# The fold's x2 rows loaded one slot of work, or one block of columns, sooner into the same two buffers

## The chip, the cores and the metric

One core of a Trainium2 chip. The metric is device time in microseconds (us) of one execution. Several runs of one kernel are told by their median and their lowest and highest.

## The reference

2,048 tokens (2 x 1,024) of width 1,024 go through two feed-forward layers, each followed by an addition of its input and a layer norm. All numbers are float32.

```python
s = silu(x @ w_gate.T)                     # 2752 columns
s[the 1376 smallest |s| of each row] = 0
x = layernorm(x + (s * (x @ w_up.T)) @ w_down.T)

def lin(x, wq, A, B):                      # wq has a quarter of the columns of w
    return x @ tile(wq, (1, 4)).T + 0.5 * (x @ A.T @ B.T)
h = silu(lin(x, w1q, a1, b1)) * lin(x, w3q, a3, b3)      # rank 2
x = layernorm(x + lin(h, w2q, a2, b2))
```

Since the second layer's weight is one block repeated four times, `x @ w.T` needs only the sum of the four quarters of `x`. That sum is the fold: four pieces of 256 columns of a row are added to one.

## The kernel before, in words

The tokens are 16 tiles of 128 rows, in four groups of four (GT). Every float32 operand is split into a high part (a cast to the matmul type) and a low part (the rest), and each product is made of three matmuls. The stages are:

- **gate_up**, to 932 us: gate and up projections of all groups, with the results stored in DRAM scratch (s_d, m_d), while topk finds the mask bytes (k_d).
- **down** (line 612), group by group: six blocks of inner columns (DB: 512, 512, 512, 384, 384, 448) times four tiles. For each block and tile, down_load (702) loads a piece m of m_d and a piece u of k_d; down_mask (725) casts u to ub on ScalarE (728) and multiplies m by it on GpSimd (729); down_prep (735) transposes m on TensorE (749), copies the high part mh on ScalarE (753) and subtracts the low part ml on VectorE (754); down_mm (778) runs the matmuls (769) and adds the result to the accumulator on VectorE (772). down_w (675) brings the block's weights: either the split pair wh, wl from scratch (688), or raw rows wr (607) that are cast on ScalarE (175) and subtracted on GpSimd (176). After the last block the accumulator is normalised and stored to x_d (793).
- Beside the **last group of down**, whose matmuls end at 1462 us, run two generators, each one step per tile of work. ffn_consts makes `br` in eight pieces of 344 columns: six tiny loads into `braw` (816) after a memset (812), a cast (175), a subtraction (176) and two small DMAs from ScalarE's queue (819). f1_first (655) does two things for t = 0 to 3: it loads the rows of tile t + 8 into an `x2a` buffer (660) for four dot products on VectorE (663), and then calls f1_tile(t) and f1_tile2(t).
- **f1_tile** (921) is the fold. It takes an x2a buffer, loads tile t's rows from x_d into it on SyncE's queue (926), adds the four quarters in three GpSimd instructions (933 to 935) into `fold`, and fills `tl` (939 to 946). **f1_tile2** (949) transposes fold and tl on TensorE (955, 957), copies to fh on ScalarE (960) and makes fl on VectorE (961). There are two x2a buffers, shared by lines 660 and 926, and one fold buffer, which line 663 also uses for its throw-away output.
- **ffn** (860), per group: eight blocks of 344 columns (NB); in blocks 0, 2, 4, 6 the folds of the next group's four tiles are made. f1_mm (964) makes the gate and up products (987 to 990), f2_prep and f2_mm the way back, layer norm and output.

The order in which an engine or a queue runs its instructions isn't that of the source. A planner that estimates durations orders them when the program is built, within the data dependences and a few orders that the source asks for: `load_behind` keeps a load behind the last load of m (714) that was issued, `behind` keeps work behind the last casts. Each engine and queue then runs its list strictly in order, and an instruction that waits holds up those behind it. Each load or store is given one of eight completion counters in turn (SyncE's and ScalarE's alike), and waits until the earlier transfer with that counter has landed; so eight are in flight at most, and a big one holds up the eighth after it.

Of the kernel before, what the change touches and what calls it, by code (L numbers as in the profile page):

```python
# [7 lines left out]
F = mybir.dt.float32  # L8
# [10 lines left out]
P = 128  # L19
H = 1024  # L20
# [5 lines left out]
NB = NI // BW  # L26
# [6 lines left out]
GT = 4  # L33
# [19 lines left out]
class Ring:  # L53
    def __init__(self, n, slots, dt):
        self.n, self.slots, self.dt = n, slots, dt
# [10 lines left out]
class Kern:  # L66
    def __init__(self, tc, A, O):
        self.tc, self.nc, self.A, self.O = tc, tc.nc, A, O
        self.nt = A["xt"].shape[0]
        self.x_seen = False  # L70
        self.lasta = self.lastv = self.lastd = None
        self.pend = self.lastp = None
        self.cache, self.wd_d, self.wd_g, self.wst = {}, {}, {}, []

    def run(self):
# [536 lines left out]
    def down(self, g, f1=None, early=0):  # L612
        n, ea = 0, []
        for ib in range(len(DB)):
            if f1 is not None:
                if ib == f1:
                    self.fg = self.f1_first()
            ws = []
            for t in range(g * GT, (g + 1) * GT):
                st = {"e": n} if n < early else {}  # L620
                load = lambda: self.down_load(st, ib, t, n)
                prep = lambda st=st, ib=ib: self.down_prep(st, ib)
                mm = lambda st=st, ib=ib, t=t, ws=ws: self.down_mm(st, ib, t, ws)
                if n < early:
                    load()
                    ea.append((self.pend, prep))
                    self.q2.append(mm)
                    if n == early - 1:
                        for j in range(2):
                            yield  # L630
                            with self.behind():
                                for e in ea:
                                    e[j]()
                        self.pend = None
                        yield
                else:
                    self.masks()
                    self.item(lambda: (load(), self.down_w(g, ib, ws)), prep, mm, 2, 3)
                n += 1
                if g == 0 and n == 12:  # L640
                    self.tkg = self.topk(self.nt // GT - 1, 2)
                if (n > 11 or g) and self.tkg and next(self.tkg, 1):
                    self.tkg, self.dg = None, self.dots_down()
                if f1 is not None and n > 4:
                    next(self.fcg, None)
                    if ib >= f1:
                        next(self.fg, None)
                for _ in range(2 if n % 2 else 1):
                    next(self.dg, None)
        if f1 is not None:  # L650
            list(self.fg)
            self.masks()
        yield

    def f1_first(self):
        for t in range(GT):
            f, x2 = self.f1_room()
            jk, o = f.bitcast(U8), t + 2 * GT
            with self.load_behind():
                self.nc.sync.dma_start(x2, self.x_d[o])  # L660
            for i in range(4):
                with self.behind():
                    self.nc.vector.scalar_tensor_tensor(
                        jk, x2, 0.5, self.abc[:, i, :], ALU.mult, ALU.mult, accum_out=self.dall[:, o, i : i + 1]
                    )
                if i < 3:
                    yield
            self.f1_tile(t, f)
            yield
            self.f1_tile2(t)  # L670
# [189 lines left out]
    def ffn(self, g):  # L860
        tiles = [t for t in range(g * GT, (g + 1) * GT) if t < self.nt]
        for b in range(NB):
            ws = []
            if tiles[-1] + 1 < self.nt:
                if b % 2 == 0:
                    if b:
                        self.f1_tile2(tiles[-1] + b // 2)
                    self.f1_tile(tiles[-1] + 1 + b // 2)
            for t in tiles:
                self.item(  # L870
                    lambda: self.f1_prep(b, ws),
                    lambda: None,
                    lambda st=self.fst[t], b=b, ws=ws: self.f1_mm(st, b, ws),
                    2, 2,
                )
        if tiles[-1] + 1 < self.nt:
            self.f1_tile2(tiles[-1] + GT)
        ws = []
        for t in tiles:
            self.item(  # L880
                lambda: self.f2_w(ws),
                lambda t=t: self.f2_prep(self.fst[t], t),
                lambda st=self.fst[t], t=t, ws=ws: self.f2_mm(st, t, ws),
                2, 1,
            )
# [20 lines left out]
    def f1_prep(self, b, ws):  # L906
        nc, fp = self.nc, self.fp
        bs = slice(b * BW, (b + 1) * BW)
        if not ws:
# [8 lines left out]
                nc.sync.dma_start(ab[:, r, :], self.A["a2"][r : r + 1, bs].partition_broadcast(P))  # L918
            ws.append(ab)

    def f1_tile(self, t, f=None):
        nc, fp, sm = self.nc, self.fp, self.sm
        V, G = nc.vector, nc.gpsimd
        st = self.fst[t] = {}
        x2 = fp.tile([P, H], F, tag="x2a", bufs=2, name="x2a")
        nc.sync.dma_start(x2, self.x_d[t])
        d = self.dall[:, t]
        f = f or fp.tile([P, 2 * P], F, tag="fold", bufs=1, name="fold")
        for i in range(4 if t >= 3 * GT else 0):
            pr = self.fp2.tile([P, H], F, tag="pr", bufs=2, name="pr")  # L930
            V.tensor_tensor(pr, x2, self.abc[:, i, :], ALU.mult)
            nc.scalar.activation(pr, pr, AF.Copy, scale=0.5, accum_out=d[:, i : i + 1])
        G.tensor_tensor(f, x2[:, 0:256], x2[:, 256:512], ALU.add)
        G.tensor_tensor(f, f, x2[:, 512:768], ALU.add)
        G.tensor_tensor(f, f, x2[:, 768:1024], ALU.add)
        dr = sm.tile([P, 4], R, tag="dr", name="dr")
        V.tensor_copy(dr, d)
        tl = fp.tile([P, P + 6], F, tag="tl", bufs=1, name="tl")
        G.memset(tl, 0.0)
        d2 = d.rearrange("p (w r) -> p w r", w=2)  # L940
        dr2 = dr.bitcast(F).rearrange("p (w r) -> p w r", w=2)
        for w in range(2):
            q = 38 * w
            V.tensor_copy(tl[:, q : q + 2], dr2[:, w])
            V.tensor_copy(tl[:, q + 2 : q + 4], dr2[:, w])
            V.tensor_tensor(tl[:, q + 4 : q + 6], d2[:, w], dr2[:, w], ALU.subtract)
        st["f"] = f, tl
# [150 lines left out]
```

## Time and profile before

| | us |
|---|---|
| runs, median (lowest to highest) | 1917.42 (1915.79 to 1919.49) |
| profiled execution, its own time | 1919.06 |
| its span, first to last instruction | 1917.3 |
| TensorE matmul busy | 1882.4 (98%) |
| VectorE, ScalarE, GpSimd busy | 1226.0, 910.2, 991.2 |
| mean granted TensorE clock | 0.994 |
| DMA moved | 485.51 MB, mean 253 GB/s |

How to read it: the first 20 us of a span of 1917.3 us and any other 20 us look alike at 98%, so the place of the missing 2% is read from tables over stretches and from the list of waits. A row of that list names the waiting engine, its operation and line, what it waited for, and then the total in us, how many times, and the longest one. In a timeline a row has its start, its duration, the engine, the line, the operation, the tiles, and in brackets the idle time before it with what ended it. SPq and ACTq are the issue of a DMA by SyncE's and ScalarE's sequencers: their time is the issue (with the gaps between merged ones), not the transfer.

### The profile page before, as it was taken

How to read it: one execution, taken by the hardware profiler on the slowest of the kernel's cores; microseconds unless marked ns; L12 is line 12 of the kernel's file. 1: busy time of each engine (PE TensorE's matmuls, PEld its weight loads, DVE VectorE, ACT ScalarE, POOL GpSimd, SP SyncE). 2: the span in 40 equal slices, each digit the busy share in tenths (PEclk: the TensorE clock that was granted, in tenths of full speed). 3: DMA queues.
4: the chain of work that ended last, by engine and by line, in shares of the span. 5: the costliest groups of instructions: out<-in, count | busy, mean ns of one | idle time of the engine just before them, and what ended most of it. 6: DMA issues, size and time to landing. Idle time of an engine off the chain costs nothing. (4 is left out here: it accounts for less than half of the span.)

```text
span 1917.3 us, 29389 instructions
## 1 busy us (share of the span) xinstructions
PE 1882.4 (98%) x10825; PEld 1752.9 (91%) x10825; DVE 1226.0 (64%) x1831; ACT 910.2 (47%) x1454; POOL 991.2 (52%) x612
## 2 busy tenths in 40 slices
PE   9999999999999999999999999999999999999998
PEld 9999999999999999999888888888777979898896
DVE  4623546667368574591249998687567857779565
ACT  4333468424783258622256633323333746567362
POOL 5665664345445344355566564543665836436062
PEclk9999999999999999999999999999999999999999
DMA  7677687676977868677687867977777878485651
GB/s 269 235 251 258 241 312 269 215 265 250 337 240 224 315 237 307 232 236 260 236 317 246 288 216 258 341 232 271 254 240 256 275 288 322 148 319 179 228 198 66
DMA packets 165341, 485.51 MB, mean 253 GB/s; under 512 B 24676, under 2 KB 45284, under 8 KB 165192
## 3 DMA queue, kind: packets, MB, share of 16 engines
q1 hardware_dynamic: 164984, 483.29, 72.4%
q8 instruction: 85, 1.39, 0.3%
q14 instruction: 64, 0.52, 0.1%
q10 hardware_dynamic: 208, 0.31, 0.0%
HBM read 367.15 MB, written 116.33 MB: 252 GB/s over the span
## 5 line engine op out<-in xcount | busy, mean ns | idle before, releaser
L176 POOL TENSOR_TENSOR wl<-wr,wh 128x1376 fp32r<-128x1376 f32 (+2 forms) x193 | 582.3, 3025 | 471.4 <-ACT wh L175 422.8
L355 PE MATMUL mm<-wh,xh 128*128 128x344 f32 x1928 | 611.0, 322 | 3.3 <-DMA wh<-tw3T1h 3.3
L355 PE MATMUL mm<-wh,xl 128*128 128x344 f32 x1928 | 610.4, 320 | 0.0
L175 ACT CAST wh<-wr 128x1376 fp32r<-128x1376 f32 (+2 forms) x198 | 238.3, 1210 | 350.9 <-PE mm L355 167.0
L355 PEld LDWEIGHTS mm<-wh,xh 128*128 128x128 f32 x1928 | 365.1, 189 | 3.6 <-issue 3.6
L355 PEld LDWEIGHTS mm<-wh,xl 128*128 128x128 f32 x1928 | 364.9, 189 | 0.0
L355 PE MATMUL mm<-wl,xh 128*128 128x344 f32 x1928 | 342.6, 320 | 0.0
L355 PEld LDWEIGHTS mm<-wl,xh 128*128 128x128 f32 x1928 | 310.8, 188 | 0.0
L769 PE MATMUL mm<-wh,mh 128*128 128x512 f32 x680 | 218.1, 401 | 0.5 <-ACT mh L753 0.5
L769 PE MATMUL mm<-wl,mh 128*128 128x512 f32 x680 | 214.6, 395 | 0.6 <-POOL wl L176 0.5
L769 PE MATMUL mm<-wh,ml 128*128 128x512 f32 x648 | 203.7, 394 | 0.8 <-DVE ml L754 0.8
L462 ACT ACTIVATE jk<-a,cur 128x2752 int8<-128x2752 f32 x66 | 170.8, 2588 | 29.0 <-DVE cur L492 19.8
L1000 POOL TENSOR_TENSOR hf<-hf,gt 128x344 f32<-128x344 f32 x96 | 142.2, 1491 | 75.3 <-DVE gt L994 68.4
L729 POOL TENSOR_TENSOR m<-m,ub 128x512 f32<-128x512 f32 (+2 forms) x93 | 112.0, 1205 | 115.7 <-ACT ub L728 63.7
L987 PE MATMUL mm<-wh,fh 128*128 128x344 f32 x512 | 166.5, 326 | 5.0 <-DVE gt L994 4.8
L989 PE MATMUL mm<-wh,fl 128*128 128x344 f32 x512 | 164.3, 321 | 0.0
L988 PE MATMUL mm<-wl,fh 128*128 128x344 f32 x512 | 164.3, 321 | 0.0
L769 PEld LDWEIGHTS mm<-wl,mh 128*128 128x128 f32 x680 | 127.0, 188 | 29.1 <-POOL wl L176 1.2
L772 DVE TENSOR_TENSOR acc<-acc,mm 128x1024 f32<-128x1024 f32 x96 | 116.5, 1213 | 54.4 <-PE mm L769 36.2
L769 PEld LDWEIGHTS mm<-wh,ml 128*128 128x128 f32 x648 | 121.1, 188 | 27.5 <-DVE ml L754 1.0
L769 PEld LDWEIGHTS mm<-wh,mh 128*128 128x128 f32 x680 | 123.5, 188 | 24.6 <-ACT mh L753 1.2
L998 ACT ACTIVATE pa<-pa 128x344 f32<-128x344 f32 x256 | 123.0, 483 | 36.4 <-DVE pa L996 31.7
(191 smaller groups left out, 2734.6 us busy)
## 6 DMA issues: line engine op xcount, KB each, us to landing
wr<-wu SPq DMA_DIRECT2D x64, 688.0 KB
wr<-wg SPq DMA_DIRECT2D x52, 688.0 KB
wr<-wd SPq DMA_DIRECT2D x54, 512.0 KB
s_d<-cc SPq DMA_DIRECT2D x64, 344.0 KB
m_d<-mt SPq DMA_DIRECT2D x64, 344.0 KB
a<-s_d SPq DMA_DIRECT2D x64, 344.0 KB
wl<-wc_w SPq DMA_DIRECT2D x48, 344.0 KB
wh<-wc_w SPq DMA_DIRECT2D x48, 344.0 KB
```

Source lines behind the costliest of these rows:

```text
L175: self.lasta = self.nc.scalar.copy(hi, raw)
L176: (eng or self.nc.gpsimd).tensor_tensor(lo, raw, hi.bitcast(F), ALU.subtract)
L355: self.nc.tensor.matmul(o, l, r, start=start and n < m and n % (2 * KH) == 0, stop=stop and n >= m and (n - m) % KH == KH - 1)
L462: nc.scalar.activation(jk.bitcast(I8), av[j], AF.Sign, bias=t, scale=-1.0, accum_out=s)
L729: nc.gpsimd.tensor_tensor(m[:, :w], m[:, :w], ub[:, :w], ALU.mult)
L769: nc.tensor.matmul(ps[:, h], a, b[:, h * 512 : (h + 1) * 512], start=i == 0, stop=i == len(ops) - 1)
L772: nc.vector.tensor_tensor(out, out, ps.rearrange("p a b -> p (a b)"), ALU.add)
L987: nc.tensor.matmul(o, fh[:, c, :], wh[:, c, :], start=c == 0, stop=False)
L988: nc.tensor.matmul(o, fh[:, c, :], wl[:, c, :], start=False, stop=False)
L989: nc.tensor.matmul(o, fl[:, c, :], wh[:, c, :], start=False, stop=False)
L998: nc.scalar.activation(pa[:, r], pa[:, r], AF.Copy, scale=0.5, accum_out=part[:, r, b : b + 1])
L1000: G.tensor_tensor(hf[:, hs], hf[:, hs], gt, ALU.add)
```

## The change

The allocation of x2a and its load leave f1_tile and become a function of their own, f1_x, which keeps the buffer in a dictionary until f1_tile takes it. The calls:

- in f1_first, f1_x(t) comes right after the load of tile t + 8, three steps ahead of f1_tile(t);
- at the end of the last down, f1_x(4);
- in ffn, f1_x for the next tile in the odd block ahead of its fold, and in block 7 for the first tile of the group after.

The load in f1_x stands in load_behind. There are still two buffers, taken in the same order, and the same 16 loads.

```diff
@@ down
         if f1 is not None:
             list(self.fg)
             self.masks()
+            self.f1_x(GT)
         yield
@@ f1_first
             with self.load_behind():
                 self.nc.sync.dma_start(x2, self.x_d[o])
+            self.f1_x(t)
             for i in range(4):
@@ ffn
                     if b:
                         self.f1_tile2(tiles[-1] + b // 2)
                     self.f1_tile(tiles[-1] + 1 + b // 2)
+                elif b < NB - 1:
+                    self.f1_x(tiles[-1] + 1 + (b + 1) // 2)
+                else:
+                    self.f1_x(tiles[-1] + GT + 1)
@@
+    def f1_x(self, t):
+        if t < self.nt:
+            self.xn[t] = self.fp.tile([P, H], F, tag="x2a", bufs=2, name="x2a")
+            with self.load_behind():
+                self.nc.sync.dma_start(self.xn[t], self.x_d[t])
+
     def f1_tile(self, t, f=None):
...
-        x2 = fp.tile([P, H], F, tag="x2a", bufs=2, name="x2a")
-        nc.sync.dma_start(x2, self.x_d[t])
+        x2 = self.xn.pop(t)
```

More of the change, by code (lines that the diff above doesn't have):

```diff
@@ L72, in __init__ @@
         self.pend = self.lastp = None
+        self.xn = {}
         self.cache, self.wd_d, self.wd_g, self.wst = {}, {}, {}, []
```

## The prediction

> **What bounds the kernel now.** The page first: it says that TensorE is the bound nearly everywhere, at full clock.
>
> ```profile
> PE 1882.4 (98%) x10825; PEld 1752.9 (91%) x10825; DVE 1226.0 (64%) x1831; ACT 910.2 (47%) x1454; POOL 991.2 (52%) x612
> PEclk9999999999999999999999999999999999999999
> ```
>
> So a change to loads can only be worth what TensorE idles near them. The table over stretches of 20 us (span; TensorE, weight loads, VectorE, ScalarE, GpSimd busy; granted clock; DMA share; GB/s) shows where that is: in the last down, where the folds of tiles 0 to 7 are made.
>
> ```profile
> 1340.00:1360.00 20.00, 20.00 (x96) 16.34 (x95) 7.96 (x9) 5.89 (x9) 11.04 (x7) 1.00 0.78 283
> 1360.00:1380.00 20.00, 16.83 (x79) 13.26 (x78) 9.26 (x14) 6.48 (x11) 12.12 (x12) 1.00 0.68 241
> 1400.00:1420.00 20.00, 18.99 (x87) 15.09 (x86) 14.75 (x22) 5.08 (x11) 11.88 (x12) 1.00 0.68 219
> 1420.00:1440.00 20.00, 18.75 (x89) 15.18 (x89) 13.63 (x24) 6.61 (x11) 12.52 (x16) 1.00 0.83 302
> 1440.00:1460.00 20.00, 17.77 (x83) 13.72 (x83) 14.13 (x36) 5.68 (x8) 12.87 (x15) 1.00 0.76 258
> 1460.00:1480.00 20.00, 17.55 (x88) 15.90 (x88) 16.05 (x51) 7.91 (x17) 11.03 (x16) 0.83 0.69 233
> ```
>
> From 1360 to 1480, TensorE lacks 10.6 us of 120 (3.17, 0.51, 1.01, 1.25, 2.23 and 2.45 by stretch; the second is not shown). The last row adds a clock of 0.83: 0.17 x 20 = 3.4 us lost besides. Next, TensorE's rows that waited, from its timeline:
>
> ```profile
> 1407.68 0.55 PE L749 MATMUL tp<-ident,m 128*128 128x128 f32 x3 [0.37 <-DVE ml L754]
> 1413.03 0.52 PE L749 MATMUL tp<-ident,m 128*128 128x128 f32 x3 [0.65 <-DVE ml L754]
> 1424.47 0.44 PE L955 MATMUL tp<-ident,fold 128*128 128x128 f32 x2 [1.25 <-POOL fold L935]
> 1451.35 0.55 PE L749 MATMUL tp<-ident,m 128*128 128x128 f32 x3 [1.16 <-DVE fl L961]
> 1472.92 0.69 PE L955 MATMUL tp<-ident,fold 128*128 128x128 f32 x2 [1.87 <-POOL fold L935]
> ```
>
> No row waits for x2a itself. The waits for fold are waits for GpSimd. What holds GpSimd is seen in SyncE's list of waits from 1376 to 1426 and in the timelines of SyncE and ScalarE:
>
> ```profile
> SPq L816 <- DMA wh<-wd2048h: 4.1, 1, 4.1
> SPq L926 <- DMA br<-braw: 2.8, 1, 2.8
> SPq L688 <- DMA x2a<-x_d: 1.5, 1, 1.5
> ```
> ```profile
> 1393.50 0.38 SPq L715 DMA_DIRECT2D u<-k_d  x1
> ...
> 1397.70 0.32 SPq L926 DMA_DIRECT2D x2a<-x_d  x1
> ...
> 1401.89 0.35 SPq L688 DMA_DIRECT2D wh<-wd1920h  x1
> ...
> 1411.37 0.35 SPq L714 DMA_DIRECT2D m<-m_d  x1
> ```
> ```profile
> 1411.82 0.48 ACT L753 CAST mh<-tp 128x384 fp32r<-128x384 f32 x1 [7.53 <-DMA wl<-wd2048l]
> ```
>
> Read them as one chain. The load of tile 2 (1397.70) waited 2.8 us for a counter. The weights wd1920 waited for that load to land (1.5 us, to 1401.89). Their four transfers landed by 1411.13 (landing records of the trace). The last tiny braw load waited 4.1 us for one of them. ScalarE's br DMA waited for another, with mh behind it, 7.53 us late. VectorE's ml follows, and TensorE stops at 1413.03. The m load at 1411.37 is late too, so its mask, the next ones and the fold behind them on GpSimd are late, and TensorE stops at 1424.47.
>
> **The change, part by part.** I number the masks of the two 384-wide blocks 1 to 8.
>
> *ffn and the end of down.* Nothing is added or removed: 16 loads of 512 KB, 0.32 us of issue each. In the orders of the two programs, SyncE's queue is the same from the w3 rows of ffn's block 0 on. The planner had already put the 12 loads of tiles 4 to 15 as early as a buffer is free. So they don't move: 0, with nothing that must hide it.
>
> *Tile 0.* Same place (1342.83): 0.
>
> *Tile 1.* Its load goes from 1382.32 to some 1376.3, ahead of two m/u pairs; its buffer is free, since fold 0 ended at 1372.9. The fold doesn't gain: it began at 1394.00, and the load had landed at 1386.45. The pairs behind get a counter later, up to 1.3 us each (u of mask 4 waits for wd1664h, landed 1382.26, instead of issuing at 1381.01). Their masks ran at 1384.58 and 1386.57, and TensorE took them at 1391.92 and 1398.24, so over 5 us of other matmuls hide it: 0. Without that cover it would cost the 1.3 us.
>
> *Tile 2, the edit that counts.* Its load now stands right behind the load of tile 10, ahead of an m and of six braw loads. Two u rows and another m that stood ahead of it (1393.50 to 1394.82) go behind the weights and twelve braw loads. The load waits for fold 1's last add, which ended at 1396.36; at 1397.70 it had waited for more than that. And by its new place the counter that wd1920 waits for is a tiny braw load's. From 1396.4: x2a and m 0.8, six braw loads 2.1 (1398.27 to 1400.33), so wd1920 issues at about 1399.3 instead of 1401.89. If fold 1 is earlier, as its masks' loads are, up to 1.5 us better still. At 1.3 us a transfer (four landed at 1.3 us steps, 1361.48 to 1365.55), with 2.9 us to the first, the weights have landed by some 1406.2 instead of 1411.13.
>
> Queued behind them is now u of mask 7: issue 1406.3, landed 2.0 us later (as the u of 1411.82 did, at 1413.83). ScalarE's list has its cast (0.51) ahead of mh of mask 5 (0.48), and then comes ml (0.56): 1409.9. TensorE needs that at 1412.4. So the waits of 0.65 and, less surely, 0.37 go. The second stands behind VectorE rows that ran 3.43 us (L663 at 1399.14, median 1.22) beside GpSimd's subtraction, so I bound it by 0 and 0.37.
>
> The fold of tile 2: GpSimd's row 933 came at 1417.76, behind a mask at 1416.76 and a braw subtraction at 1412.98 that waited for ScalarE. These move up by about 3 us. VectorE's last dot product (1415.54 to 1416.79) still bounds it. From there the three adds and what lies between took 6.65 us, 1.15 of it a wait for the next u: end 1422.3 to 1423.4 instead of 1424.41. TensorE asked at 1423.22, less what was gained before. So 0.5 to 1.25 of that wait goes. Sum for tile 2: 1.2 to 2.3 us; I take 2.2, because the trace has the whole chain moving by more than each wait is long.
>
> *Tile 3.* Its load in fact moves a place later, behind a row of w3. It landed at 1434.12, the fold began at 1442.65: 0, with 8 us of cover.
>
> *Behind it, 1448 to 1453.* TensorE waited 0.25, 1.16 and 0.77 for ScalarE and VectorE, which were at the splits of the w3 and w1 rows (ScalarE idle 7.97 us for these, until 1446.53). If those rows come as much earlier as TensorE does, the waits stay: 0. If the loads gain more, all 2.18 go. If they gain less, it may cost as much as TensorE gained, 2.2. The loads stand behind the same backlog, which begins 2 to 3 us earlier, so I take the middle of the first two: 1.1.
>
> *At 1470 to 1473* the wait stays. One fold buffer makes tile 6's transposes, three adds (2.3 us) and tile 7's transposes a row of steps, and tile 7's load was issued at 1460.23. [...] The trace differs: with gaps of 0.39 and 1.87 the clock fell to 0.83 of 20 us, while 1.69 and 1.48 between 1360 and 1380 left it at 1.00. [...]
>
> **Sum.** 2.2 + 1.1 = 3.3 us. The profiled execution took 1919.06 us, its span 1917.3 with 1.8 around it: it would take 1915.8. It stands 1.6 us above the median of the runs. From the median, 1917.42 - 3.3 = 1914.1.
>
> **The rivals.**
>
> *The u row comes too late (slower).* The saving hangs on wd1920 moving up. If it stays at 1401.89, because the fold, the braw memsets on GpSimd or a counter hold SyncE's queue as long as before, the weights land at 1411.13, u of mask 7 at 1413.2, and then 0.51, 0.48 and 0.56 give ml at 1414.8. ScalarE's cast of u has blocked mh behind it. TensorE waits from 1412.8 (the planner put two more matmuls ahead): 2.0 instead of 0.65, so 1.3 more. A stall of 2 us may also halve the clock as at 1472, another 3.4: 1917.42 + 4.7 = 1922.1, or 1918.7 without. It decides when that u lands after about 1411.3. For it: ScalarE's queue is strict, and u gives up a lead of 12 us. Against it: the waits of 2.8 and 1.5 us that vanish.
>
> [...]
>
> *The change does nothing (same).* The gain is given back in ffn's first group, where the DMA queues are near full and TensorE already waits 2.83 us at 1546.57 for ScalarE: 1917.4, give or take 1.5. Against it: that wait stands in a chain of ScalarE, VectorE and GpSimd work that moves along with TensorE.
>
> **How the numbers follow.** About 0.2% (3.8 us) is what a measurement of this kernel can tell from no change; faster ends at 1913.6, slower begins at 1921.3. Main case 0.40, own range 1912.3 to 1915.8: 0.17 faster, 0.23 same. Late u row 0.27: 0.21 slower, 0.06 same. Clock case 0.15, all faster. Nothing 0.18, all same. Together 0.32, 0.47 and 0.21. The range reaches from 1910.3, about the middle of the clock case, to 1922.2, the far price of the late u row.
>
> **What would show it.** Right: wd1920 issued by 1399.5 or so, no wait of line 688 for x2a, the 7.53 of line 753 and TensorE's 0.65 and 1.25 gone, and the ffn stretches as before, only earlier. Wrong: line 728 of ScalarE waiting for u near 1411 with mh behind it, a longer wait of line 749, or a granted clock below 1.00 between 1400 and 1440. The clock row of 1460 to 1480 tells the third case. I would be most wrong if the planner's new order makes another engine's list wait where I followed only SyncE's.

## The result, and the profile after

| | before | changed |
|---|---|---|
| median (lowest to highest), 22 runs each, taken together | 1916.69 (1911.59 to 1919.99) | 1919.65 (1912.12 to 1927.18) |
| ratio, 95% interval | | 1.0019 [1.0010, 1.0028] |
| profiled execution, its own time (span) | 1919.06 (1917.3) | 1920.05 (1918.2) |

The change makes the kernel 0.19% slower. The forecast was 3.3 us less; it became about 3 us more. The page shows almost nothing: TensorE's busy time is the same, and the clock row has an 8 in one slice (1439 to 1487 us).

```profile
PE 1882.7 (98%) x10825; PEld 1753.0 (91%) x10825; DVE 1229.8 (64%) x1831; ACT 910.7 (47%) x1454; POOL 988.2 (52%) x612
PEclk9999999999999999999999999999998999999999
```

The table over stretches says where. These are the rows that were shown of before:

```profile
1360.00:1380.00 20.00, 17.00 (x81) 13.23 (x80) 9.76 (x17) 7.06 (x12) 13.55 (x13) 1.00 0.72 250
1400.00:1420.00 20.00, 20.00 (x93) 16.30 (x93) 14.17 (x23) 5.67 (x12) 11.60 (x14) 1.00 0.84 270
1420.00:1440.00 20.00, 18.95 (x90) 15.02 (x89) 12.92 (x23) 5.22 (x9) 11.62 (x11) 1.00 0.70 266
1440.00:1460.00 20.00, 15.88 (x69) 12.04 (x68) 13.72 (x35) 6.07 (x8) 10.14 (x14) 0.91 0.70 255
1460.00:1480.00 20.00, 17.52 (x88) 15.88 (x87) 15.09 (x49) 7.51 (x16) 11.03 (x17) 0.83 0.61 211
```

Between 1400 and 1420 TensorE no longer idles (20.00 for 18.99), as forecast. Between 1440 and 1460 it loses 1.9 us more than before (15.88 for 17.77), and the clock, which was 1.00 there, is 0.91: another 0.09 x 20 = 1.8 us.

Stretches of fixed time shift against the work, so I also count from the same matmul to the same matmul. The piece of work that before runs from 1446.0 to 1462.1 us (the 8,269th to the 8,332nd matmul of the record) took 16.1 us in that profile and 17.5 in a second one of before; in two profiles of the changed kernel it took 19.1 and 19.2. So about 2.3 of the 3 us are lost within this piece. (Up to it, the changed kernel's two profiles stood 2.8 us ahead on average, but 2.6 of that is half clock near 882 us (0.5 granted), in both profiles of before (a mean of 0.83 and 0.91 between 880 and 900 us) and in neither of these (1.00 in the first). Two other kernels with the loads early (further on) have it too, 0.91 with the split behind the add and 0.83 with the casts moved as well, and before with the casts moved has 1.00, so it does not go with the change.) TensorE's timeline shows the waits behind this:

```profile
1446.79 0.73 PE L772 MATMUL mm<-wh,mh 128*128 128x512 f32 x2 [0.93 <-ACT mh L756]
1450.40 0.55 PE L752 MATMUL tp<-ident,m 128*128 128x128 f32 x3 [2.41 <-DVE fl L973]
1451.28 0.73 PE L772 MATMUL mm<-wh,ml 128*128 128x512 f32 x2 [0.23 <-DVE ml L757]
...
1473.02 0.69 PE L967 MATMUL tp<-ident,fold 128*128 128x128 f32 x2 [1.88 <-POOL fold L947]
```

At the same three tiles before waited 0.25, 1.16 and 0.77; now it is 0.93, 2.41 and 0.23. The wait of 1.87 at 1472.92 is still there and just as long. VectorE's timeline of before, and then that of the changed kernel, tell why the 1.16 doubled:

```profile
1443.53 1.22 DVE L772 TENSOR_TENSOR acc<-acc,mm 128x1024 f32<-128x1024 f32 x1 [1.96 <-PE mm L769]
1448.00 1.78 DVE L176 TENSOR_TENSOR wl<-wr,wh 128x688 fp32r<-128x688 f32 x1 [3.25 <-ACT wh L175]
1449.70 1.27 DVE L578 BATCH_NORM_STATS2 bn<-acc 128x6 f32<-128x512 f32 x2
1450.90 0.40 DVE L961 TENSOR_TENSOR fl<-tp,fh 128x256 fp32r<-128x256 f32 x1
```
```profile
1445.80 1.77 DVE L177 TENSOR_TENSOR wl<-wr,wh 128x688 fp32r<-128x688 f32 x1 [4.70 <-ACT wh L176]
1447.49 1.21 DVE L775 TENSOR_TENSOR acc<-acc,mm 128x1024 f32<-128x1024 f32 x1
1448.73 1.29 DVE L579 BATCH_NORM_STATS2 bn<-acc 128x6 f32<-128x512 f32 x2
1449.94 0.41 DVE L973 TENSOR_TENSOR fl<-tp,fh 128x256 fp32r<-128x256 f32 x1
```

The two lists hold the same work in another order. `wl` here is the low part of w3's rows for ffn's first group (block 1, called the split below). It needs ScalarE's cast, and the cast needs the rows from DRAM. In before the add of the last block's first tile ran ahead of it, while VectorE would have waited anyway. Now the add, 1.21 us, stands behind it, and with it bn and fl, which releases the tile that TensorE transposes into. ScalarE has the same bottleneck, with mh behind two casts:

```profile
1444.34 1.44 ACT L176 CAST wh<-wr 128x688 fp32r<-128x688 f32 x2 [9.09 <-DMA wr<-w]
1445.68 0.58 ACT L972 CAST fh<-tp 128x512 fp32r<-128x512 f32 x1
1446.15 0.59 ACT L756 CAST mh<-tp 128x512 fp32r<-128x512 f32 x1
```

In before the casts began at 1446.53 after 7.97 us of idle. So the rows of w came 2.2 us earlier, while TensorE stood 2.9 us further on (its transposes of the fold at 1442.46, before at 1445.38). The source asks for none of this: the planner made a new list for every engine because a few loads had moved. Of the lead that TensorE had won, the rows lacked 0.7 us, which is about what the wait for mh grew by (0.93 for 0.25).

### The profile page after: what moved, and what is told of

The parts are those of the page before. It is cut to its first block, busy times and chain, and to the rows that moved or that the text cites. A ratio compares the mean times of both kernels' runs of the same rounds, so it can differ in the third digit from the quotient of the medians.

```text
span 1918.2 us, 29384 instructions
## 1 busy us (share of the span) xinstructions
PE 1882.7 (98%) x10825; PEld 1753.0 (91%) x10825; DVE 1229.8 (64%) x1831; ACT 910.7 (47%) x1454; POOL 988.2 (52%) x612
```

## Experiments

All times are against the kernel before, run beside. I also use two sums, taken the same way for every kernel. The *waits* are the idle times that TensorE's timeline shows before rows that begin between 1436 and 1456 us, in the one profiled execution. The *clock part* of a run is (1 - its mean granted clock) x its span, as a mean over the runs of a kernel; the clock is given to 0.001 (1.9 us), so only means over many runs are of use. The theories: A, the new order of VectorE's list costs the time; B, TensorE merely comes earlier to a place that the weight rows set; C, the loss is elsewhere.

**Before again, unchanged.**

> The kernel before, unchanged, for the mean clock of its single runs: all theories expect a ratio of 1.000. If the scatter of the runs is half-clock windows, 0.001 of mean clock goes with 1.9 us.

Measured: 1917.19 us, 0.9999 [0.9990, 1.0007]. Its profile is worth more than its time. From 1380 to 1436, where I had found the tile 2 gain, TensorE's waits were these:

```profile
PE mm L769 <- POOL wl L176: 0.3, 1, 0.3
```

In the execution that I had read, they were 2.78 us. Over six profiles with the loads where before has them, they are 2.78, 0.27, 0.79, 0.43, 1.01 and 0.47; over six with the loads early, 1.03, 0.72, 0.51, 1.74, 0.85 and 1.87. (The two kernels with two fold buffers are left out: they have another order here, and 2.15 and 2.46 us.) The means are 0.96 and 1.12, each good to about 0.4. Before's second profile has one more such wait just past the stretch, 1.48 us at 1439.7; counted on to where the wait for mh begins, the means are 1.4 and 1.6. On average there was nothing like 2.2 us to gain. The 1.25 for fold stands in none of the other five profiles of the first kind, and the 0.65 for ml has at most a 0.43 in its place.

**The changed kernel again, unchanged.**

> The changed kernel again, unchanged, for a second profile and twelve more times. The waits that the order makes (fl near 2.4 us and mh near 0.9 us, between 1446 and 1451 us) should come again in every execution; waits that are a matter of one execution (near 1428 us, and the half clock at 882 us) should not. Ratio to before 1.0010 to 1.0028.

Measured: 1920.62 us, 1.0019 [1.0010, 1.0028]. The waits do come again:

```profile
1444.08 0.72 PE L772 MATMUL mm<-wh,mh 128*128 128x512 f32 x2 [1.04 <-ACT mh L756]
1447.68 0.55 PE L752 MATMUL tp<-ident,m 128*128 128x128 f32 x3 [2.42 <-DVE fl L973]
```

**The split put behind the add** (before's order at this place of VectorE's list).

```diff
-        self.split(wh, wl, wr, self.nc.vector if ...)
+        self.split(wh, wl, wr, self.nc.vector if ...,
+                   after=self.add12 if key == ("w3", 1) else None)   # add12: first tile of the last block
```

> The changed kernel, with the VectorE subtraction of the w3 rows of block 1 put behind the add of the last block's first tile, as it stood before the change (on VectorE only these two rows change places). Theory A (the new VectorE order costs the time): the TensorE wait for fl near 1450, 2.41 us after the change, falls to about 1.2, the half-clock window at 1452 goes in most runs, and the ratio to before is 0.999 to 1.000. Theory B (TensorE merely comes earlier to a place that the arrival of the weight rows sets): the wait stays at 2 us or more and the ratio at about 1.002. Theory C (the loss is elsewhere): wait gone or not, the ratio stays at 1.002.

Measured: 1918.24 us, 1.0008 [0.9999, 1.0018]. The wait for fl fell from 2.41 to 1.14, about before's 1.16; the 0.88 for mh stayed, and 0.59 for ml came.

```profile
1448.32 0.62 PE L753 MATMUL tp<-ident,m 128*128 128x128 f32 x3 [1.14 <-DVE fl L976]
```

The half clock did not go: 6.8 us of it begin at 1448.7 in this profile (0.83 between 1440 and 1460). As means over the runs, the edit took 1.5 ± 0.8 us off the changed kernel's time and left 1.8 ± 0.7 above before (table further on). So A explains perhaps half of the loss. What is left is ScalarE's wait, B, or something elsewhere.

**The casts on ScalarE moved behind mh as well** (of the last block's third tile).

```diff
+                   after=self.add12 if key == ("w3", 1) else None,
+                   cast=self.mhs[-2] if key in (("w1", 1), ("w3", 1)) else None)
```

> The changed kernel, with ScalarE's casts of the w1 and w3 rows of block 1 put behind the copy mh of the last block's third tile, and the VectorE subtraction behind the add as in the run beside it. Theories A and B both: the TensorE waits of 0.93 (mh) and 2.41 (fl) near 1446 to 1450 vanish, no half clock there, and the 2 us gained between 1400 and 1425 are kept: ratio 0.9975 to 0.999. Theory C: ratio stays at 1.002.

Measured: 1913.74 us, 0.9990 [0.9980, 1.0000], so the loss is gone and some more. ScalarE now runs fh and mh first, and TensorE's stretch from 1440 to 1460 is nearly full (19.46 of 20), at full clock:

```profile
1446.99 0.59 ACT L978 CAST fh<-tp 128x512 fp32r<-128x512 f32 x1 [7.91 <-PE tp L975]
1447.48 0.59 ACT L758 CAST mh<-tp 128x512 fp32r<-128x512 f32 x1
1448.25 1.44 ACT L177 CAST wh<-wr 128x688 fp32r<-128x688 f32 x2 [0.18 <-DMA wr<-w]
```
```profile
1440.00:1460.00 20.00, 19.46 (x95) 15.89 (x94) 19.04 (x42) 5.22 (x8) 12.97 (x15) 1.00 0.76 259
```

The expectation gave A and B the same outcome here, so the time can't choose between them. The rows still come only at 1448, and TensorE no longer waits: it did not need them yet, only what stood behind them. B in its plain form falls with this. That the rows gained 0.7 us less than TensorE still counts, but by way of the queue.

**The same edit on the kernel before.**

> The kernel before, with the same edit as in the changed kernel with the casts moved: ScalarE's two casts of the weight rows of block 1 (w1, w3) behind the mh copy of the last block's third tile, VectorE's split of w3 behind the accumulator add. If the queueing behind these casts is a price that both kernels pay, and the earlier loads only raised it, this version gains as well: before's waits near 1448 us (0.25, 1.16, 0.77) go, 1.5 to 2.2 us, ratio 0.9990 to 0.9995. If the casts matter only in the order that the earlier loads made, ratio 1.0000 (within 0.0005) or above. If it gains as much as the changed kernel does by the edit (5.4 us), the earlier loads were worth nothing in themselves.

Measured: 1912.71 us, 0.9978 [0.9967, 0.9990]. So before pays for the same queueing, and more than I had thought. This is the fastest version, ahead of both kernels. By the means it gains 4.2 ± 0.6 us, against 5.6 ± 0.8 by the same edit in the changed kernel. But here the edit changes TensorE's own list too, from 1458 us on, which it does not in the changed kernel, so the gain is not that of the casts alone. In its profile the pair of waits near 1471 us, 0.39 and 1.87, became a single 2.34, and the clock beside it stayed at 1.00.

**One instruction on another engine.** A cleaner edit: in the changed kernel the subtraction alone goes to GpSimd. The lists of TensorE and ScalarE are then the changed kernel's own. (The planner also reorders some twenty rows of VectorE behind this place, and on GpSimd the subtraction stands ahead of a fold.)

```diff
-    self.nc.vector if key[0] == "w3" or key in (...) else None
+    self.nc.vector if (key[0] == "w3" and key[1] != 1) or key in (...) else None
```

> The changed kernel with one instruction on another engine: the subtraction of w3's block 1 (128x688) runs on GpSimd and no longer on VectorE, so that nothing of VectorE's list stands behind the weight rows; TensorE's and ScalarE's orders are the changed kernel's own. If the cost of the change is VectorE's queueing behind this subtraction, TensorE's wait of 2.41 us for fl at 1450 us falls to 0 to 0.5 us, the wait of 0.93 us for mh (ScalarE, behind the casts) stays, and the time falls by 2 to 4 us: ratio to before 0.9998 to 1.0009. If TensorE merely comes earlier to a place that the weight rows set, the wait moves to another tile near by and the ratio stays at 1.0015 to 1.0025. A third way: GpSimd takes the subtraction ahead of a fold that TensorE waits for, and the time rises.

Measured: 1916.29 us, 0.9999 [0.9987, 1.0010]. Against before as it is, the whole loss is gone. The 2.41 for fl is 0, the 0.88 for mh stays, and VectorE takes the add as soon as it can:

```profile
1440.10 2.34 DVE L775 TENSOR_TENSOR acc<-acc,mm 128x1024 f32<-128x1024 f32 x2
1442.48 1.29 DVE L579 BATCH_NORM_STATS2 bn<-acc 128x6 f32<-128x512 f32 x2
...
1446.46 0.42 DVE L973 TENSOR_TENSOR fl<-tp,fh 128x256 fp32r<-128x256 f32 x1 [2.45 <-ACT fh L972]
```

Both adds run back to back from 1440.10, so in the changed kernel the add that began at 1447.49 could have begun at about 1441. It stood 6 us behind an instruction that it has nothing to do with.

The gain is not free. At the fold of tile 6 TensorE now waits for GpSimd, which it did in neither kernel:

```profile
1467.08 0.44 PE L967 MATMUL tp<-ident,fold 128*128 128x128 f32 x2 [1.85 <-POOL fold L947]
```

From 1436 to 1480 us the waits are 5.5, against 6.4 and 7.0 in the two profiles of the changed kernel. The other part that can be seen is the clock, 1.00 from 1440 to 1460 here and 0.91 there.

**The same instruction moved in before.**

> The kernel before with the same edit that took the loss from the changed kernel (0.9999 of before): the subtraction of w3's block 1 runs on GpSimd. In before one accumulator add stands ahead of this subtraction, not behind it, but bn and fl stand behind it all the same (wait for fl 1.16 us, ml 0.77 us at 1450 us). If the loss of the changed kernel is the greater wait behind this instruction and nothing else, both kernels should be level once it is gone: 0.9985 to 1.0000 here, the changed kernel within 0.001 of it. If the earlier loads cost something of their own as well, this version stands 0.0015 or more below the changed kernel with the same edit: 0.9984 or less.

Measured: 1914.29 us, 0.9987 [0.9975, 0.9999]. A wait of 1.61 for fold at 1467 comes here as well. The edit in both kernels gives a table of means (± standard error; for before, of the runs whose clock is on record):

| us | loads as before | loads early | difference |
|---|---|---|---|
| split on VectorE | 1916.72 ± 0.22 (126 runs) | 1920.02 ± 0.49 (33) | +3.3 ± 0.5 |
| split on GpSimd | 1914.82 ± 0.71 (12) | 1916.74 ± 0.60 (11) | +1.9 ± 0.9 |

With the instruction where it stood, the changed kernel pays 3.3 ± 0.8 us for it, and before 1.9 ± 0.7. The early loads save nothing in either row. What the new order adds is the difference between the two, 1.4 ± 1.1 us, not clear of zero; it agrees with the 1.5 ± 0.8 of the split put behind the add, though both are counted from the same runs of the changed kernel. With the instruction moved in both kernels, 1.9 ± 0.9 us of the early loads' cost stay. The wait of 0.88 for mh, which in the two profiles only the changed kernel has, is the part of this that can be seen; the rest is open. The ratios, 0.9987 and 0.9999, are 0.0012 apart, where the expectation asked for 0.001 or 0.0015: they don't settle whether VectorE's wait is the whole loss.

With the casts moved in both, the difference is 1.9 ± 0.9 us again (1914.44 less 1912.53), though neither profile has a wait for mh, fl or ml; there it is clock part, 9.9 ± 0.4 for 7.2 ± 0.3, and TensorE's lists differ.

**The subtraction made twice, and four times, in before.**

> The kernel before, with the same subtraction made twice (the second writes the same values), so that VectorE has 1.7 us more ahead of fl near 1450. Theory A: the TensorE wait for fl grows from 1.16 to about 2.8 us, a half-clock window joins it in many runs, ratio 1.001 to 1.0025. Theory B: the same wait, but since it is VectorE work and not the rows' arrival that is added, it says only what a stall here costs: 1.6 us, ratio 1.001. Theory C: ratio 1.000.

> The kernel before, with the subtraction of w3's block 1 made four times (the same result each time), so that VectorE's list behind it comes about 3 us later. Made twice it raised the wait for fl from 1.16 to 2.13 us and cost nothing that could be measured (1.0001). If a stall at this place passes to the end, and calls up half clock as it grows, the wait rises to about 4 us and the time by 3 to 6 us: 1.0015 to 1.0030. If what follows (the fold at 1471 us) absorbs the stall, within 0.0007 of 1: then the loss of the changed kernel isn't this stall.

Measured: 1917.11 us, 1.0001 [0.9992, 1.0010], and 1918.33 us, 1.0008 [0.9996, 1.0020]. The wait for fl became 2.13 and 2.14: the planner put other work between the copies, so four cost TensorE hardly more than two, and the dose I wanted was never given. As a test of size these two are weak.

**Ten idle matmuls in the changed kernel's gap**, to see whether idle time itself calls up the half clock.

> The changed kernel, with ten more matmuls of 128x128 whose result nobody reads, put behind the products of the last block's second tile, so that TensorE has work (ten by about 0.06 to 0.11 us) where it idles for 2.41 us at 1450 us; the order that makes the wait stays. It asks whether TensorE's idle time itself costs the clock. If idle time within a few microseconds of TensorE calls up the half clock, the idle time that is left (about 1.3 to 1.8 us) is too little: the half clock at 1452 us goes and the time falls by 1 to 2 us below the changed kernel, ratio to before 1.0009 to 1.0014. If the clock doesn't hang on this stall, the ten matmuls cost nothing or up to 1 us: 1.0019 to 1.0025.

Measured: 1921.24 us, 1.0023 [1.0009, 1.0036], which decides nothing. The gap was not filled: TensorE ran most of the ten first, from 1446.70 to 1448.65, and then waited 2.84 us for fl, and a half clock of 3.4 us followed at 1452.9 (0.91 between 1440 and 1460). So the clock part, which fell from 11.3 ± 0.4 to 8.5 ± 0.6 us, can't be laid on this gap. And the rest of the time rose by 4.6 us (1908.7 to 1913.3). The lists of all engines changed, and in ffn's first group the wait for gt grew from 1.4 to 4.5:

```profile
PE mm L1004 <- DVE gt L1011: 4.5, 4, 2.2
```

**Two fold buffers**, in before, and in the changed kernel with the casts moved. (Room for it was made by giving three small topk and statistics tiles fewer buffers.)

> The kernel before, with two buffers for fold in place of one. The wait of 1.87 us at 1471 us (TensorE's transposes behind the fold of GpSimd) goes if that wait is for the buffer; if the half clock of 6.8 us that begins with it (3.4 us lost) hangs on the wait, this goes too: 1.9 to 5.3 us, ratio 0.9972 to 0.9990. If the half clock comes anyway, at most 1.9 us: 0.9990. If the fold itself is late and not its buffer, nothing: within 0.0005 of 1.

> The changed kernel with both edits: casts behind mh, and two buffers for fold. If the two stalls (1446 to 1451 us, and 1471 us) are separate and each carries its own half clock, the gains add: casts alone stand at 0.9990 of before, the second buffer gives another 1.9 to 5.3 us, so 0.9962 to 0.9980. If the second buffer gives nothing, 0.9990. If the scheduler's order is broken elsewhere by the second buffer, above 0.9990.

Measured: 1913.88 us, 0.9988 [0.9976, 1.0001], and 1914.05 us, 0.9988 [0.9977, 0.9999]. The first may gain 2.3 us, but not in the way expected: the wait for fold at 1471 gave way to waits of 1.82 and 1.03 for tl, and the half clock there stayed (0.83). On top of the casts the second buffer gave nothing (e3 has 0.9990). The stall at 1471 is thus not one of the buffer alone. Where the first one's gain lies stays open; its order differs on all five engines, TensorE's from 1379 us on.

**All together.** The waits of one profile beside the mean time of the kernel's runs:

| kernel | waits, us | mean time, us |
|---|---|---|
| before, casts behind mh | 0.00 | 1912.53 ± 0.52 |
| changed, casts behind mh | 0.54 | 1914.44 ± 0.68 |
| before, split on GpSimd | 0.47 | 1914.82 ± 0.71 |
| changed, split on GpSimd | 1.43 | 1916.74 ± 0.60 |
| before (two profiles) | 2.18, 3.42 | 1916.72 ± 0.22 |
| before, subtraction twice | 2.82 | 1917.51 ± 0.73 |
| before, four times | 3.18 | 1918.28 ± 0.75 |
| changed, split behind the add | 3.03 | 1918.57 ± 0.64 |
| changed (two profiles) | 4.12, 4.22 | 1920.02 ± 0.49 |

In this table the time follows the waits: over these eleven profiles the correlation is 0.94, the slope 1.5 us per us. Three kernels that also changed other things are left out, and don't all fit: idle matmuls 3.38 and 1921.79, two folds 2.89 and 1914.39, two folds with casts 3.93 and 1913.95. With them the correlation is 0.65. The last has nearly the changed kernel's waits and is 6 us faster, so the sum of the waits at this place does not fix the time.

## Why the prediction was wrong

*SyncE's part was right.* wd1920 was forecast for about 1399.3 and was issued at 1398.61, with an m and six braw loads between it and tile 2's load:

```profile
1393.36 0.35 SPq L932 DMA_DIRECT2D x2a<-x_d  x1
...
1398.61 0.35 SPq L691 DMA_DIRECT2D wh<-wd1920h  x1
```

The wait of line 688 for x2a is gone, and so is the 7.53 us of mh, which came at 1408.87 for 1411.82. The late u row did not happen: no TensorE row waits between 1400 and 1420. That tiles 0, 1 and 3 and all of ffn are worth 0 agrees too. A program with only the ffn calls of the change has before's order on all five engines, and one with only the f1_first calls has the changed kernel's; these two orders were compared, not run. In the profiles all that follows 1462 us took 455.2 and 455.1 us in before, 456.0 and 454.7 in the changed kernel.

*"Tile 2, the edit that counts": 2.2 us. This term failed.* The mechanism ran as told, but the waits that it takes away were in one execution only: 2.78 us there, 0.96 on average over six profiles, and 1.12 with the loads early. The gain is 0, within about half a microsecond. One profile was taken for the kernel.

*"Behind it, 1448 to 1453": 1.1 us of gain. This is the step that turned the sign.* In its place the work there took 2.3 us more (19.1 for 16.8 as means of two profiles, the clock included). I had asked whether the rows of w gain as much as TensorE does, and bounded the cost at 2.2 us. I took the middle of the two better cases; the rows gained 2.2 us and TensorE 2.9, the third case. What I had not done was to read VectorE's and ScalarE's new lists at this place, as I had read SyncE's. The add stands behind the split there: that was to be seen in the order of the two programs. The three waits named in this step (mh, fl and ml together) went from 2.18 and 1.94 us in the two profiles of before to 3.57 and 3.69 in those of the changed kernel. I named this danger in my last sentence and gave it no case.

*The clock.* The 3.4 us at 1472 were left in, and they stayed (0.83 in the first profile of either kernel). That they would go, the clock case with its chance of 0.15 and its part in the range, was an estimate of mine that no run of the changed kernel shows: between 1460 and 1480 its two profiles have 0.83 and 0.91, those of before 0.83 both times, and of all fourteen only that of before with the casts moved has 1.00. What I had left out is half clock beside the stall at 1450: 0.91 between 1440 and 1460 in both profiles of the changed kernel, and in one of the two of before. Over all fourteen profiles, half clock begins between 1446 and 1454 us in eight of the ten that have 2.2 us or more of waits from 1436 to 1456 (0.83 to 0.91 between 1440 and 1460), and in none of the four that have less than 1.5 (1.00).

*The sum as measured.* The rest of the time, without the clock part, rose from 1907.4 ± 0.2 to 1908.7 ± 0.3, by 1.3, against 1.6 us more of the three waits. The clock part rose from 9.4 ± 0.2 to 11.3 ± 0.4, by 2.0. Together 3.3 us, where the forecast had -3.3. Where most of it is lost (2.3 us) is shown by two profiles of each kernel. Why is shown in part: VectorE's new order makes the wait for fl longer (2.41, 1.14 with the old order at this place, 0 with the split on GpSimd) and is worth 1.4 ± 1.1 or 1.5 ± 0.8 us by the two edits that took it away. The other 1.9 us stay in the runs with those edits. The longer wait for mh behind ScalarE's casts is a part of them, argued from the traces and not tested by itself. That the waits also make the clock part is likely, not shown: with next to no waits here in either kernel (0.00 and 0.54) the clock part was 7.2 in before with the casts moved and 9.9 in the changed kernel with them, so something else moves it as well, and filling the gap did not work.

## What to carry to other kernels

When a planner orders the work, a moved load makes a new list for every engine. Read each of them around the place where TensorE waits, above all for an instruction that waits on DRAM with work behind it that doesn't. Before a wait in a trace is booked as a gain, look whether a second execution of the same kernel has it. To test whether such an instruction is the cost, give it to another engine with as few other lists changed as can be, and do the same in the kernel before: the first edit alone seemed to explain the whole loss, and the second showed that before pays a part of the same price. And follow the waits past the place of the edit, since some of what is saved there can come back at the next thing that TensorE waits for: here 1.85 us for fold at 1467, with the split on GpSimd.

## What the runs showed of the hardware

- The clock goes with a part of the scatter between runs. Over the 33 runs of the changed kernel (1912.12 to 1927.18 us, granted clock 0.996 to 0.991) time and clock correlate at -0.82; over the 126 runs of before whose clock is on record, at -0.56. The slopes are 1.9 and 1.4 us for 0.001 of clock; one thousandth of the span is 1.9.
- In the clock records of the first profile of either kernel the granted clock is 1.00 from 4.8 us on but for pieces at 0.5: four of 3.4 us, three of 6.8 us, and one of 6.7 or 7.5 us with which each execution ends. Between 1440 and 1480 us the half clock came with these waits, among others: 0.93, 2.41 and 0.23 within 5 us in the first profile of the changed kernel (3.4 us of it from 1452.0), 1.04, 2.42 and 0.23 in the second (0.91 between 1440 and 1460). It did not come with such waits every time: 1.17 and 0.77 us were followed by 3.4 us of it in one execution of before, 1.16 and 0.77 by none up to 1472 in the other. A wait of 2.34 us at 1462 (before with the casts moved) left the clock at 1.00, and one of 2.35 at 1473.6 (the run with the idle matmuls) came with 3.4 us of it (0.91 between 1460 and 1480). What decides it, the runs do not say.
